# Three shared-expert parts moved to the last batch's end, second choices' sends written behind the shared expert, last norms in four groups

## The chip, the cores and the metric

The kernel runs on one core of a Trainium2 chip. The metric is the device time of one execution in microseconds (us); lower is better. TensorE is written PE, VectorE DVE, ScalarE ACT, GpSimd POOL and SyncE SP.

## The reference

One decoder layer for B = 4 batches of S = 1024 tokens of H = 256 features, float32 throughout, with a layer norm after each of three sublayers:

```python
x = _layernorm(x + self_attention(x))              # 16 heads, blended with two 4-head attentions
x = _layernorm(x + cross_attention(x, ctx, dist))  # 154 keys, a bias from log(dist)
x = _layernorm(x + moe(x))

# moe(h), 4096 tokens:
probs  = softmax(h @ gate_w)                       # 8 experts
w, idx = top_k(probs, 2); w = w / w.sum()          # two choices a token
y      = sum over the two choices: w * expert_idx(h)
y     += (silu(h @ ws_gate) * (h @ ws_up)) @ ws_down   # the shared expert, width 512
```

An expert has the form of the shared one: a gate and an up product of width 512, silu, and a product down to 256.

## The kernel before, in words

Tokens lie on the 128 partitions; a batch is NT = 8 tiles of 128 tokens, `ys[b]` is `[128, 8, 256]`. The four batches are worked through one after the other: self-attention, `close_sublayer` (output product, residual add, statistics, norm), the cross-attention's loop of 36 steps (`Cross.scores`, `flip`, `product`), and `end` (the cross-attention's `close_sublayer`, the transposes of the normed tokens, L135 with the copy L138, and the router's scores, L856, copied to `prob` at L863). Only then are all 4096 tokens routed.

Work that other engines leave room for is written as Python generators and stepped from inside these loops. `ahead` is such a generator: for batches 0 to 2 it holds the beginning of the next batch's self-attention (`begin`); in the last batch it is `shared_early(2)`, the shared expert for batch 2. `shared` yields 13 parts, called p0 to p12 here: p0 transposes the tokens, p1 to p4 are gate and up products of the first 512 tokens (L191), p5 to p8 those of the second 512, p9 to p12 the products down (L174), each followed by an add (L888) and a DMA to DRAM (L891). In the last batch p0 and p1 are stepped after the two `out_features` products, the others from `close_sublayer` and the cross loop, as the idle yields in `shared_early` space them.

Routing is a chain of small DVE operations (L1142 to L1239). It gives each of the 2 x 4096 choices a place in a DRAM array `scratch`, grouped by expert. `send(b, k)` writes two columns (`tail`: the token's number and the choice's weight) behind the 256 features in the tile `sent[b]` (`[128, 8, 258]`), and POOL then issues eight indirect DMAs, one for each tile of tokens, which scatter these rows to their places. Batches 0 and 1 have been kept in DRAM and are read again for that (`y0again`, `y1again`); in the profile `y` stands for batches 2 and 3. There are two rounds, k = 0 and k = 1; the second overwrites the two columns in the same tile. While that goes on, PE runs the shared expert for batch 0, batch 1 and the first half of batch 3 (`begin_result`), whose transposes read `sent[b][:, :, 0:H]`.

Then 72 tiles of 128 places are read back (`fetch`), go through their expert (`hidden`, `flip`, `down`) and are added to `result` by an indirect DMA. At the end `res[b]` is loaded from DRAM (L1397), the second half of batch 3's shared expert (`rest`) is finished on chip, and the last norm runs: `bn_stats` and `bn_aggr` on DVE (L1405, L1406), the square root on ACT (L1412), and the apply on ACT (L1422) or DVE (L1426), with one output DMA for each part (L1429).

The order of instructions on each engine is set by a scheduler from the order in which the program writes them; waits between engines are semaphores that the framework places by tile. [...]

Of the kernel before, what the change touches and what calls it, by code (L numbers as in the profile page):

```python
# [20 lines left out]
NT = S // P  # L21
# [19 lines left out]
def run(gen):  # L41
    for _ in gen:
        pass
# [3 lines left out]
def decoder_layer(ctx: ExitStack, tc: tile.TileContext, a, out):  # L47
# [53 lines left out]
    def rows(b):  # L101
        return result[b * S : (b + 1) * S, :].rearrange("(t p) d -> p t d", p=P)
# [57 lines left out]
    def shared(y, room, gated, add, together):  # L160

        x2T = room("x2T", [P, NC2, S])
        transpose_tokens(x2T, y)
        yield

        def down(tb, hid):
            for tp in range(2):
                ps = small()  # L170
                for i in range(2):
                    tok = 2 * tp + i
                    for f in range(NF):
                        nc.tensor.matmul(  # L174
                            ps[:, i * H : (i + 1) * H],
                            hid[:, f, tok * P : (tok + 1) * P],
                            shared_weights(2 * NC2 * D + f * H, H),
                            start=(f == 0),
                            stop=(f == NF - 1),
                        )  # L180
                add(ps, tb * 4 + 2 * tp)
                yield

        pend = []
        for tb in range(2):
            hid = room(f"hid{tb}", [P, NF, 512])
            for f in range(NF):
                ps = big()
                for i in range(2):
                    for c in range(NC2):  # L190
                        nc.tensor.matmul(  # L191
                            ps[:, i, :],
                            shared_weights((i * NC2 + c) * D + f * P, P),
                            x2T[:, c, tb * 512 : (tb + 1) * 512],
                            start=(c == 0),
                            stop=(c == NC2 - 1),
                        )
                gated(hid[:, f, :], ps)
                yield
            pend.append((tb, hid))  # L200
            if tb == 1 or not together:
                while pend:
                    yield from down(*pend.pop(0))


    with tc.tile_pool(name="wA", bufs=1) as wA, tc.tile_pool(name="work", bufs=2) as work:
# [581 lines left out]
        def close_sublayer(y, product):  # L788

            mv = work.tile([P, NT, nc.vector.BN_AGGR_DIM], F32, tag="mv", name="mv")  # L790
            for t in range(0, NT, 2):
                ps = small()
                for i in range(2):
                    product(ps[:, i * H : (i + 1) * H], slice((t + i) * P, (t + i + 1) * P))
                yy = y[:, t : t + 2, :]
                nc.vector.tensor_tensor(yy, ps.rearrange("p (t d) -> p t d", d=H), yy, ALU.add)
                ln_stats(y, t, mv, work)
                ln_stats(y, t + 1, mv, work)
                yield
            rstd = ln_rstd(mv, work, 0, NT)  # L800
            for t in range(NT):
                ln_apply(y, t, mv, rstd, t)
                if t % 2 == 1:
                    yield
# [67 lines left out]
        def shared_early(b):  # L872

            tags = {"x2T": "xT", "hid0": "v16", "hid1": "v64"}

            def room(name, shape):
                return work.tile(shape, F32, tag=tags[name], name="s" + name, bufs=1)

            def gated(dst, ps):

                sg = work.tile([P, 512], F32, tag="avs", name="sg")
                nc.scalar.activation(sg, ps[:, 0, :], AF.Tanh, scale=0.5)
                nc.vector.scalar_tensor_tensor(sg, sg, 1.0, ps[:, 0, :], ALU.add, ALU.mult)
                nc.vector.scalar_tensor_tensor(dst, ps[:, 1, :], 0.5, sg, ALU.mult, ALU.mult)

            def add(ps, t0):
                so = work.tile([P, 2, H], F32, tag="avs", name="so")
                nc.vector.tensor_tensor(  # L888
                    so, ps.rearrange("p (t d) -> p t d", d=H), ys[b][:, t0 : t0 + 2, :], ALU.add
                )  # L890
                nc.sync.dma_start(rows(b)[:, t0 : t0 + 2, :], so)  # L891

            for n, _ in enumerate(shared(ys[b], room, gated, add, True)):
                yield
                if n > 4:

                    yield
                    yield

        run(begin(0))  # L900

# [21 lines left out]
        for b in range(B):  # L923
# [82 lines left out]
                        ps, cm[:, c, tok], wo[:, c, :], start=(c == 0), stop=(c == NC2 - 1)  # L1006
                    )

            for _ in close_sublayer(y, self_out):
                next(ahead, None)  # L1010


            cT = work.tile([P, NC2, S2], F32, tag="cT", name="cT", bufs=1)
# [55 lines left out]
            for n in range(total + 4):  # L1069
                if n < total:  # L1070
                    xa.scores(n)
                    if n % 8 == 3 and n // 8 < NG - 1:
                        xa.project_q(n // 8 + 1)
                if 2 <= n < total + 2:
                    xa.flip(n - 2)
                if n >= 4 and n % 2 == 1:
                    xa.product(n - 4)
                next(ahead, None)
                xa.clock.step()
            xa.clock.finish()  # L1080
            cx4 = work.tile([P, NC2, S], F32, tag="cx", name="cx4", bufs=1)
            run(to_features(xtok, cx4, 1.0))
            run(ahead)
            behind = end(b, cx4)
            if b == B - 1:
                run(behind)


    NTT = B * NT
# [150 lines left out]


    def send(b, k):
        nc.gpsimd.tensor_copy(sent[b][:, :, H:RW], tail[:, k, b * NT : (b + 1) * NT, :])
        for t in range(NT):
            g = b * NT + t
            ins = nc.gpsimd.indirect_dma_start(
                out=scratch[:, :],
                out_offset=bass.IndirectOffsetOnAxis(ap=place[:, k, g : g + 1], axis=0),
                in_=sent[b][:, t, :],
                in_offset=None,  # L1250
            )
            tc.declare_no_dep(ins.ins, group="send", reason="places are unique")
            tc.add_to_no_dep_group("send", ins.ins)
# [91 lines left out]
        nc.scalar.activation(sl, ps[:, 0, :], AF.Silu)  # L1345
        nc.vector.tensor_tensor(dst, ps[:, 1, :], sl, ALU.mult)

    for k in range(2):
        for b in (2, 3, 0, 1):
            send(b, k)  # L1350

# [15 lines left out]
    for b in (0, 1):  # L1369
        run(begin_result(b, True))  # L1370
        nc.sync.dma_start(rows(b), res[b])
    b = B - 1
    nc.sync.dma_start(rows(b)[:, NT // 2 :, :], ys[b][:, NT // 2 :, :])
    rest = begin_result(b, False)
# [22 lines left out]
        nc.sync.dma_start(res[b], rows(b))  # L1397


    def statistics(parts, n):  # L1400
        mv = fw.tile([P, 16, nc.vector.BN_AGGR_DIM], F32, tag="mv", name="mv", bufs=3)
        for k, (b, t0) in enumerate(parts):
            for t in range(n):
                st = fw.tile([P, nc.vector.BN_STATS_DIM], F32, tag="bnst", name="bnst", bufs=3)
                nc.vector.bn_stats(st, res[b][:, t0 + t, :])  # L1405
                nc.vector.bn_aggr(mv[:, k * n + t, :], st)  # L1406
            yield mv

    def norm(parts, n, mv):
        m = n * len(parts)  # L1410
        rstd = fw.tile([P, 16], F32, tag="rstd", name="rstd", bufs=3)
        nc.scalar.activation(rstd[:, :m], mv[:, 0:m, 1], AF.Sqrt, bias=eps_t)  # L1412
        nc.vector.reciprocal(rstd[:, :m], rstd[:, :m])
        off = fw.tile([P, 16], F32, tag="off", name="off", bufs=3)
        nc.vector.scalar_tensor_tensor(
            off[:, :m], mv[:, 0:m, 0], -1.0, rstd[:, :m], ALU.mult, ALU.mult
        )
        for k, (b, t0) in enumerate(parts):
            for t in range(n):
                y, i = res[b][:, t0 + t, :], k * n + t  # L1420
                if i % 2 == 0:
                    nc.scalar.activation(  # L1422
                        y, y, AF.Identity, bias=off[:, i : i + 1], scale=rstd[:, i : i + 1]
                    )
                else:
                    nc.vector.tensor_scalar(  # L1426
                        y, y, rstd[:, i : i + 1], off[:, i : i + 1], ALU.mult, ALU.add
                    )
            nc.sync.dma_start(od[b][:, t0 : t0 + n, :], res[b][:, t0 : t0 + n, :])  # L1429

    halves = [(b, t) for b in range(B) for t in (0, NT // 2)][:-1]
    groups = [halves[:4], halves[4:]]
    stats = [statistics(g, NT // 2) for g in groups]
    mvs = [None, None]
    for f in range(NF):
        next(rest)
        g = stats[f // 2]
        for _ in range(2):
            mvs[f // 2] = next(g, mvs[f // 2])
    norm(groups[0], NT // 2, mvs[0])  # L1440
    norm(groups[1], NT // 2, mvs[1])
    for t0 in (NT // 2, NT // 2 + 2):
        next(rest)
        part = [(B - 1, t0)]
        norm(part, 2, next(statistics(part, 2)))
    run(rest)


# [27 lines left out]
```

## Time and profile before

| what | us |
|---|---|
| median of three runs | 3334.01 (3328.59 to 3344.21) |
| profiled execution | 3394.53 |
| its span | 3392.7 |
| PE busy | 3215.2 (95%) |
| DVE, ACT, POOL busy | 1670.2, 1612.6, 353.5 |
| mean granted PE clock | 0.973 |

The profile records one execution. A row of the timeline gives start and duration in us, then engine, line, operation, output and inputs, and in brackets the engine's idle time ahead of it with what ended it. A row of the waits gives the waiting instruction, what it waited for, the total, the number of times and the longest. A row of the windows gives for each stretch its length, the busy time and count of PE, its weight loads, DVE, ACT and POOL, the granted clock, the share of busy DMA engines and GB/s.

### The profile page before, as it was taken

How to read it: one execution, taken by the hardware profiler on the slowest of the kernel's cores; microseconds unless marked ns; L12 is line 12 of the kernel's file. 1: busy time of each engine (PE TensorE's matmuls, PEld its weight loads, DVE VectorE, ACT ScalarE, POOL GpSimd, SP SyncE). 2: the span in 40 equal slices, each digit the busy share in tenths (PEclk: the TensorE clock that was granted, in tenths of full speed). 3: DMA queues.
4: the chain of work that ended last, by engine and by line, in shares of the span. 5: the costliest groups of instructions: out<-in, count | busy, mean ns of one | idle time of the engine just before them, and what ended most of it. 6: DMA issues, size and time to landing. Idle time of an engine off the chain costs nothing.

```text
span 3392.7 us, 60480 instructions
## 1 busy us (share of the span) xinstructions
PE 3215.2 (95%) x25064; PEld 2047.2 (60%) x25064; DVE 1670.2 (49%) x3512; ACT 1612.6 (48%) x3168; POOL 353.5 (10%) x569
## 2 busy tenths in 40 slices
PE   8999999999999999999999999999999992999997
PEld 3655666566556665665576666555766761666664
DVE  3665555566645555666465555664555550111113
ACT  1555544465655444756554356655453630233333
POOL 1000000000000010000000100000000025133331
PEclk7999999999999999999999999999999996999999
DMA  7200000110000001100000100000000052122224
GB/s 230 76 2 1 1 1 3 45 35 31 2 1 1 1 18 36 45 15 2 1 1 1 38 16 21 14 2 11 1 10 1 14 203 91 41 46 46 47 44 120
DMA packets 83768, 111.36 MB, mean 33 GB/s; under 512 B 8896, under 2 KB 69672, under 8 KB 83496
## 3 DMA queue, kind: packets, MB, share of 16 engines
q1 hardware_dynamic: 70056, 89.60, 8.4%
q0 software_dynamic: 13440, 17.90, 3.2%
q8 instruction: 200, 3.28, 0.4%
q14 instruction: 72, 0.59, 0.1%
HBM read 59.10 MB, written 48.37 MB: 32 GB/s over the span
## 4 chain that ended last, share of the span: by engine, by line
PE 82%; DVE 10%; issue 3%; another core or an unknown queue 2%; ACT 1%; DMA 1%; POOL 0%; SPq 0%; DVEq 0%; POOLq 0%; ACTq 0%
PE big L483 8%; PE big L591 8%; PE big L1292 7%; PE one L627 7%; PE acc L645 7%; DVE mxp L490 7%; PE big L342 7%; PE one L541 7%; PE one L521 4%; PE acc L1318 4%; PE one L758 3%; PE big L191 3%; PE one L356 3%; PE big L723 3%; PE acc L777 2%
## 5 line engine op out<-in xcount | busy, mean ns | idle before, releaser
L490 DVE TENSOR_REDUCE mxp<-big 128x2 f32<-128x1024 f32 x512 | 610.8, 1219 | 347.5 <-PE acc L521 261.6
L483 PE MATMUL big<-k,q 31*128 31x512 f32 x2048 | 616.4, 639 | 34.3 <-DVE mxp L490 23.9
L521 PE MATMUL one<-q,k 32*128 32x256 f32 x2784 | 502.0, 398 | 0.0
L532 ACT ACTIVATE ex<-one 128x512 f32<-128x512 f32 x696 | 390.8, 600 | 220.5 <-PE acc L521 178.9
L323 DVE CUSTOM_DVE_ANT_0 prob<-big,zero_t 128x1024 f32<-128x1024 f32 x256 | 303.6, 1222 | 271.5 <-PE big L591 271.3
L521 PEld LDWEIGHTS one<-q,k 32*128 32x128 f32 x2784 | 331.6, 186 | 33.8 <-issue 2.5
L610 ACT ACTIVATE prob<-prob,nmx 128x1024 f32<-128x1024 f32 x256 | 293.0, 1152 | 21.9 <-DVE nmx L323 21.4
L483 PEld LDWEIGHTS big<-k,q 31*128 31x128 f32 x2048 | 186.3, 188 | 175.6 <-DVE mxp L490 88.8
L591 PE MATMUL big<-mk,mq 64*128 64x512 f32 x1024 | 284.0, 632 | 2.1 <-ACT ex L529 2.0
L632 ACT COPY pt<-one 128x512 f32<-128x512 f32 x256 | 137.8, 589 | 308.8 <-PE one L627 308.8
L627 PEld LDWEIGHTS one<-ident,prob 128*128 128x128 f32 x2048 | 220.4, 141 | 97.5 <-issue 91.8
L1292 PE MATMUL big<-wall,xt 128*128 x576 | 270.4, 593 | 0.5 <-ACT xt L1271 0.5
L521 PE MATMUL acc<-q,k 32*128 32x256 f32 x928 | 264.6, 404 | 0.0
L627 PE MATMUL one<-ident,prob 128*128 128x128 f32 x2048 | 256.3, 278 | 0.0
L541 PE MATMUL one<-ex,v 128*32 128x256 f32 x4096 | 250.9, 385 | 5.0 <-DVE q L400 5.0
L743 ACT ACTIVATE xs<-xs,xmx 128x154 f32<-128x154 f32 x512 | 175.1, 414 | 114.9 <-DVE xmx L323 114.9
L1302 DVE TENSOR_TENSOR hidr<-big,slr 128x512 f32<-128x512 f32 x72 | 49.8, 691 | 364.5 <-ACT slr L1300 364.5
L541 PEld LDWEIGHTS one<-ex,v 128*32 128x32 f32 x4096 | 120.2, 110 | 139.2 <-ACT ex L532 54.0
L634 DVE COPY pt<-one 128x512 f32<-128x512 f32 x256 | 164.3, 683 | 9.8 <-PE one L627 9.8
L591 PEld LDWEIGHTS big<-mk,mq 64*128 64x128 f32 x1024 | 99.8, 190 | 101.6 <-issue 79.5
L323 DVE CUSTOM_DVE_ANT_0 xs<-big,bias 128x154 f32<-128x154 f32 x512 | 132.6, 314 | 51.7 <-ACT avx L785 25.3
L554 POOL TENSOR_TENSOR avq<-avq 128x256 f32<-128x256 f32 x64 | 46.5, 726 | 1055.3 <-ACT avq L549 1055.3
(258 smaller groups left out, 4698.0 us busy)
## 6 DMA issues: line engine op xcount, KB each, us to landing
scratch<-empty SPq DMA_DIRECT2D x1, 9288.0 KB
xg<-scratch SPq DMA_DIRECT2D x72, 129.0 KB
q<-q_rows SPq DMA_DIRECT2D x16, 512.0 KB
k<-k_rows SPq DMA_DIRECT2D x16, 512.0 KB
y<-in_x_dram SPq DMA_DIRECT2D x4, 1024.0 KB
q_rows<-qh SPq DMA_DIRECT2D x8, 512.0 KB
k_rows<-kh SPq DMA_DIRECT2D x8, 512.0 KB
wall<-in_L_ffn_w_gate_dram SPq DMA_DIRECT2D x8, 512.0 KB
```

What stands on the lines that cost most here:

```text
L323: nc.vector.tensor_tensor_reduce(out=out, in0=ps, in1=bias, scale=-1.0, scalar=3.0e38, op0=ALU.add, op1=ALU.min, accum_out=low,)
L342: nc.tensor.matmul(ps[:, tb, :], w[:, c, lo : lo + P], xT[:, c, tb * 512 : (tb + 1) * 512], start=(c == 0), stop=(c == NC2 - 1),)
L483: nc.tensor.matmul(ps[:, jj, :], st["q"][r : r + MR, tok : tok + P], st["k"][r : r + MR, kb * 512 : (kb + 1) * 512], start=True, stop=True,)
L490: nc.vector.reduce_max(mxp[:, t, kb, 2 * pair : 2 * pair + 2], ps, axis=AX.X)
L521: nc.tensor.matmul(scs[jj][:, i * QW : (i + 1) * QW], st["k"][r : r + MR + 1, kc * P : (kc + 1) * P], st["q"][r : r + MR + 1, part * QW : ...
L532: nc.scalar.activation(ex[:, jj, :], scs[jj], AF.Exp, scale=1.0 / HD**0.5)
L541: nc.tensor.matmul(av[32 * j : 32 * j + 32, 0:QW], self.v[:, kc, h * VW : h * VW + 32], exs[kc // 2, j // 2][:, j % 2, i : i + QW], start= ...
L591: nc.tensor.matmul(pss[i][:, kb, :], q[r : r + MD, t * P : (t + 1) * P], k[r : r + MD, kb * 512 : (kb + 1) * 512], start=True, stop=True,)
L610: nc.scalar.activation(p, p, AF.Exp, bias=nmx[:, i : i + 1], scale=-1.0, accum_out=sm[:, t % 4, i : i + 1],)
L627: nc.tensor.transpose(ps[:, kc * P : (kc + 1) * P], probs[u][i][:, at : at + P], ident)
L645: nc.tensor.matmul(av[64 * i : 64 * i + 64, (t % 4) * P : (t % 4 + 1) * P], v[:, kc, h * MD : (h + 1) * MD], flipped[u][i][:, kc, :], star ...
L1292: nc.tensor.matmul(ps[:, g, :], xt[:, c * P : (c + 1) * P], wall[:, bass.ds(off + (g * NC2 + c) * D, D)], start=(c == 0), stop=(c == NC2 - 1),
```

## The change

Three parts of the program are changed.

A. `shared_early` returns the generator of `shared` itself, without idle yields. In the last batch `close_sublayer` steps it at every second yield (p2 to p5), the cross loop at n = 6, 12, 18 and 24 (p6 to p9), and `end` at its yields 4, 6 and 8 (p10 to p12). For the other batches the stepping stays as it was.

B. `send` copies the first choices' columns on DVE instead of POOL. Before the shared expert the program now writes only the first choices' sends; those of the second choices follow behind the shared expert of batches 0 and 1, for batches 2, 0, 3, 1.

C. The last norms are made in four groups of two half batches (8, 8, 8 and 4 tiles) where there were two of four and three, each with its statistics directly ahead of it. One tile in four is applied on DVE and three on ACT; before it was every second. In the two parts of batch 3's last half it stays one of two. The last four gate parts of the shared expert are written ahead of all of it and no longer interleaved with the statistics.

```diff
@@ shared_early
-            for n, _ in enumerate(shared(ys[b], room, gated, add, True)):
-                yield
-                if n > 4:
-
-                    yield
-                    yield
+            return shared(ys[b], room, gated, add, True)
@@ the loop over batches
-            for _ in close_sublayer(y, self_out):
-                next(ahead, None)
+            for n, _ in enumerate(close_sublayer(y, self_out)):
+                if b < B - 1 or n % 2 == 0:
+                    next(ahead, None)
@@
-                next(ahead, None)
+                if b < B - 1 or n in (6, 12, 18, 24):
+                    next(ahead, None)
                 xa.clock.step()
@@
-            run(ahead)
             behind = end(b, cx4)
             if b == B - 1:
-                run(behind)
+                for n, _ in enumerate(behind):
+                    if n > 3 and n % 2 == 0:
+                        next(ahead, None)
+            run(ahead)
@@ send
-        nc.gpsimd.tensor_copy(sent[b][:, :, H:RW], tail[:, k, b * NT : (b + 1) * NT, :])
+
+        eng = nc.gpsimd if k else nc.vector
+        eng.tensor_copy(sent[b][:, :, H:RW], tail[:, k, b * NT : (b + 1) * NT, :])
@@
-    for k in range(2):
-        for b in (2, 3, 0, 1):
-            send(b, k)
+    for b in (2, 3, 0, 1):
+        send(b, 0)
@@
     for b in (0, 1):
         run(begin_result(b, True))
         nc.sync.dma_start(rows(b), res[b])
+    for b in (2, 0, 3, 1):
+        send(b, 1)
@@ the last norms
-    def statistics(parts, n):
+    def norm(parts, n, on_dve):
         mv = fw.tile([P, 16, nc.vector.BN_AGGR_DIM], F32, tag="mv", name="mv", bufs=3)
...
-            yield mv
-
-    def norm(parts, n, mv):
+
         m = n * len(parts)
...
-                if i % 2 == 0:
+                if i % on_dve:
                     nc.scalar.activation(
@@
-    groups = [halves[:4], halves[4:]]
-    stats = [statistics(g, NT // 2) for g in groups]
-    mvs = [None, None]
-    for f in range(NF):
+    for _ in range(NF):
         next(rest)
-        g = stats[f // 2]
-        for _ in range(2):
-            mvs[f // 2] = next(g, mvs[f // 2])
-    norm(groups[0], NT // 2, mvs[0])
-    norm(groups[1], NT // 2, mvs[1])
+    for k in range(0, len(halves), 2):
+        norm(halves[k : k + 2], NT // 2, 4)
     for t0 in (NT // 2, NT // 2 + 2):
         next(rest)
-        part = [(B - 1, t0)]
-        norm(part, 2, next(statistics(part, 2)))
+        norm([(B - 1, t0)], 2, 2)
     run(rest)
```

## The prediction

> **What bounds the kernel now.** I read the page first (busy time by engine, busy slices, chain), then went into the three stretches that the change touches with the windows, the chain, the waits and the timeline. Two rows of the page's slices carry the first reading:
>
> ```profile
> PE   8999999999999999999999999999999992999997
> ...
> POOL 1000000000000010000000100000000025133331
> ...
> PE 82%; DVE 10%; issue 3%; another core or an unknown queue 2%; ACT 1%; DMA 1%; POOL 0%; SPq 0%; DVEq 0%; POOLq 0%; ACTq 0%
> ```
>
> PE sets the time: 3215.2 us busy of 3392.7. One slice, the 34th, breaks it with a 2 (each is 84.8 us, so it runs from 2799 to 2884), and it is the slice in which POOL is busiest. The waits between 2780 and 2870 us name the hole:
>
> ```profile
> ACT x2T L138 <- remote: 78.1, 2, 56.7
> PE big L191 <- ACT x2T L138: 42.9, 1, 42.9
> PE big L191 <- issue: 20.3, 1, 20.3
> DVE res L1360 <- issue: 25.3, 3, 20.4
> ```
>
> PE loses 42.9 + 20.3 = 63.2 us there waiting for two copies on ACT. What do those copies wait for? The timelines of PE, ACT, DVE and POOL:
>
> ```profile
> 2796.59 1.91 PE L135 MATMUL big<-ident,y1again 128*128 128x128 f32 x16
> ...
> 2840.31 1.01 ACT L138 COPY x2T<-big 128x1024 f32<-128x1024 f32 x1 [56.74 <-remote]
> 2862.71 1.01 ACT L138 COPY x2T<-big 128x1024 f32<-128x1024 f32 x1 [21.39 <-remote]
> ...
> 2797.53 0.69 DVE L1360 TENSOR_TENSOR res<-one,y0again 128x512 f32<-128x512 f32 x1 [6.96 <-PE one L174]
> 2818.61 0.69 DVE L1360 TENSOR_TENSOR res<-one,y0again 128x512 f32<-128x512 f32 x1 [20.39 <-issue]
> ...
> 2850.73 0.21 POOL L1243 COPY y1again<-tail 128x16 f32<-128x16 f32 x1
> 2860.15 0.97 POOL L1246 DMA_INDIRECT scratch<-y1again,place  x1 [0.30 <-issue]
> ```
>
> PE's transposes of y1again were through by 2798.5, yet the copies that only need them start at 2840.31 and 2862.71; the last down product of batch 0 was through near 2796.6, and its add starts at 2818.61. Four uses of PE's results in a row come 21.1, 21.7 and 22.4 us apart, while POOL issues 64 indirect sends back to back (2779.07 to 2861.1, 1.275 us each: 0.97 busy and 0.30 issue); once the last send is out it is over. No k=1 copy of `tail` stands in it: y1again's columns are written at 2850.73, 54 us after PE had started to read that tile. So the tail copies are not what these four wait for.
>
> Is this hole in the timed runs? The profiled execution took 3394.53 us (span 3392.7 and 1.8 around it), the median of the runs is 3334.01: 60.5 less. PE's rows without the hole end this stage 62.8 us earlier (2866.4 for 2929.2), which gives 3331.7, inside the runs' 3328.6 to 3344.2. I take it that the hole belongs to the profiled execution and that timed runs mostly lack it. This is the main choice of the forecast; the other reading is a rival below.
>
> **Part A: three parts of batch 2's shared expert moved to the last batch's end.** A part is 3.43 us of PE (L191, eight matmuls) or 3.45 (L174, eight). Before: p2 to p6 in `close_sublayer`, p7 to p12 in the cross loop. After: p2 to p5, then p6 to p9, and p10 to p12 in `end`. Both earlier places have PE full (48.83 busy of 50 us from 2560 to 2610; 118.36 of 122 from 2610 to 2732), so a part taken out is worth its whole length: −3.43 in `close_sublayer` (one less), −6.87 in the loop (net two less), less 0.2 us of start-up idle that p7 at n=1 filled. In `end` the three cost +10.35, of which this much lies in gaps:
>
> ```profile
> 2742.81 4.02 PE L135 MATMUL big<-ident,y 128*128 128x128 f32 x16 [2.88 <-DVE y L126]
> ...
> 2742.34 2.67 DVE L126 TENSOR_SCALAR y<-y,mv,rstd 128x256 f32<-128x256 f32 x8
> ```
>
> PE idles 2.88 us for the first normed tile, and its 16 transposes, paced by DVE's applies, take 4.02 where 16 unpaced take 1.91: 5.0 us of cover. Sum: −3.43 − 6.87 + 0.2 + 10.35 − 5.0 = −4.8 us (−3 if p10 alone fills, −5 at best). What is issued with them: three DVE adds (0.69 each, L888) and three 256 KB output DMAs on SP. On DVE one add stands between the reciprocal (L122) and the applies and waits for p10, two between the applies and the probability copy (L863); each is done before the PE scores (L856) behind p12 are. The third add also waits for the first part's DMA to leave its buffer. On SP they stand ahead of the expert-weight loads, which need the released buffer anyway and end near 2780, 80 us before an expert uses them.
>
> Behind it the routing keeps its order on DVE, but ACT now runs the routing softmax (L1144) between batch 0's two x2T copies: prob is 1.7 us earlier, the second copy later by two table loads. PE's first gate part pays +0.8 and the rank products (L1171/1172) wait where they ran free before: +1.05 net. A comes to −4.8 + 1.05 = −3.75 us on PE, and the sends start about 7.9 us earlier.
>
> Here a rule bears: by the trace a table load is 1.28 us (2754.99) with 0.02 us between the neighbour's end and it; the Trainium skill's "ScalarE: Activation LUTs", section "What ACT_TABLE_LOAD costs", adds a drain of about 1.38 us to each, 2.66 in all. One drain more ahead of the second copy would make A about −2.4; the rows show none, and I keep −3.75.
>
> **Part B: second choices sent behind the shared expert's code, the first ones' tail copies on DVE.** 64 sends before, 64 after, 1.275 us each, in another order; nothing on POOL stands between the two sets, since the k=1 copies have no reader to wait for. POOL loses four copies of 0.2 to 0.33 us; DVE gains four (nearest row: its 128x16 copies of L1186 at 0.17 us), 0.7 us in all ahead of the first shared products. First rule against it: the Trainium skill's "SBUF — State Buffer", section "SBUF: two separate sides", says that an fp32 SBUF-to-SBUF copy on DVE locks GpSimd out of the port with which it writes descriptors. Row: the sends keep 1.275 us under all of DVE's work from 2779 to 2819, though none of that is such a copy. By the rule the sends of y2 lose at most the other three copies, 0.5 us; by the row none. The first expert's gather (xg) lands 3.6 us after the last send (2864.7) and would be 7.9 us earlier; without the hole PE gets there at 2866.4. So B is worth 0 (−0.5 to +0.5), covered by PE's shared products; without that cover the send chain would be the bound, and it ends earlier too.
>
> **Part C: last norms in four groups, three quarters of the tiles on ACT.** Before, the output DMAs start late and then run at one rate:
>
> ```profile
> 3374.00:3376.00 2.00, 0.33 (x2) 0.30 (x3) 2.00 (x10) 0.00 (x0) 0.00 (x0) 1.00 0.00 0
> ...
> 3388.00:3390.00 2.00, 0.00 (x0) 0.00 (x0) 0.00 (x0) 0.00 (x0) 0.00 (x0) 0.50 1.09 385
> ...
> 3377.63 6.97 ACT L1422 ACTIVATE res<-res,off,rstd 128x256 f32<-128x256 f32 x14
> 3378.73 9.37 SPq L1429 DMA_DIRECT2D out_dram<-res  x9
> ```
>
> 4.19 MB from 3379.6 to 3390.5 at about 383 GB/s: the queue is the bound, its start is what counts. After: eight tiles' statistics (0.39 each on DVE) from 3365.0, sqrt, a Silu reload (1.28) and the last Silu (0.6), then six applies (0.498) on ACT: the first write near 3374.0, 5.6 us earlier. But ACT then has 23 applies (11.5 us) where it had 16, two table loads more (2.6 us), and waits for group 1's offsets, which stand on DVE behind 24 tiles of statistics (3378.55). Its last apply ends near 3387.85; 0.85 us from issue to data (as 3378.73 to 3379.6), 0.7 of data and the same tail put the end at 3389.5 to 3391. ACT takes the queue's place: C = 0 (−3 to +3; +2.7 with the page's drain at each of the two loads). DVE, with 9 applies where it had 16, is no cover for it.
>
> **The sum.** −3.75 + 0 + 0 = −3.75 on 3394.5, carried over to the median: 3334.0 − 3.8 = **3330 us**. Half a percent is 16.7 us, about what a measurement of this kernel can tell from no change.
>
> **Rivals.**
> - *As summed*, −12 to +8: chance 0.50.
> - *It doesn't do what it says*: the k=1 copies had nothing to wait for, p11 and p12 cover no idle time and the routing waits eat the rest: 3334, 0.14. For it: the copy at 2850.73. Against: 5.0 us of gap.
> - *The hole is real in the timed runs and goes.* For it: it stands in the one execution that the records show, and no load of instructions falls in it; fewer PE results have to reach other engines inside an earlier send train. Against: the 60.5 us difference, and that all 64 sends stay back to back. One late result less is −21 − 4: 3309; two, −42 − 4: 3288; all of it, −63 − 4: 3267. Faster, 0.22.
> - *A late result in the timed runs, slower.* The same delay, one mechanism, in a place where timed runs now escape it: x2T's copy (L138) of y1again or of batch 3's half while sends run. Moving the train 8 us against DVE and PE can let one result in; price 21 − 4 = +17 (3351), two +38 (3372). It decides from a delay of 20.5 us on. Against it: the median without a hole fits. 0.14.
>
> **Numbers.** Faster by over 0.5% 0.22, within it 0.64, slower 0.14. The range takes one late result either way and leaves out the larger ones: 3306 to 3356; the likeliest case alone is 3322 to 3342.
>
> **What would show.** A: PE's idle before the last L135 group of the batch under 1 us, 8 shared matmuls in it, probability copy 3 to 5 us earlier. B: 64 sends at 1.275 us, ordered k=0 then k=1 as before, no wait at the k=1 copies. C: first output DMA near 3374 of the old scale, ACT busy to the end. I am wrong if the timed median moves by more than 17 us, or if POOL's k=1 copies turn out to wait for PE.

## The result and the profile after

The changed kernel takes 3323.9 us (median of 20 executions, 3315.9 to 3334.9); the kernel before takes 3337.3 beside it. The ratio is 0.9965 (95% interval 0.9955 to 0.9975), so 8 to 15 us less. The forecast was 3330 us and 3.8 us less: the time lies in its range and within its half percent, but the gain is about three times as large as the sum said.

The two spans, 3392.7 and 3314.1 us, must not be compared as they stand. The hole of the profile before is not in the profile after. Slices of its page, and its chain:

```profile
PE   8999999999999999999999999999999999999997
...
POOL 1000000100000001000000010000000004433331
...
PE 84%; DVE 10%; issue 3%; ACT 2%; DMA 1%; POOL 0%; SPq 0%; ACTq 0%; DVEq 0%; POOLq 0%
```

PE has no slice with a 2, and no "unknown queue" stands in the chain, with POOL as busy as before. The waits of the changed kernel between 2780 and 2870 us, the same stretch in which PE lost 63.2 us before:

```profile
ACT x2T L138 <- PE big L135: 28.2, 2, 14.1
PE big L191 <- ACT x2T L138: 0.5, 2, 0.2
```

ACT's copies wait for their transposes alone, and PE for the copies 0.5 us. Was that the change? The experiments say no. Part A shows in PE's timeline at the end of the last batch:

```profile
2719.63 3.62 PE L844 MATMUL one<-xwo,cx 128*128 128x256 f32 x16
2723.09 7.07 PE L174 MATMUL one<-shwmc,shid 128*128 128x256 f32 x32
2729.99 1.04 PE L135 MATMUL big<-ident,y 128*128 128x128 f32 x8
2730.87 3.62 PE L174 MATMUL one<-shwmc,shid 128*128 128x256 f32 x16
2734.32 1.04 PE L135 MATMUL big<-ident,y 128*128 128x128 f32 x8
2735.20 0.29 PE L856 MATMUL one<-gw,x2T 128*128 128x8 f32 x2
```

None of these rows has an idle time in brackets. Where PE had waited 2.88 us for the norm and then been paced by it, it now works on the shared expert's products down (L174), and the 16 transposes run unpaced.

To see what a part is worth, I measure every profile from one point, the first self-output product of the last batch (L1005, L1000 after the change); all before it is the same program in each of these kernels. It begins anywhere between 2576 and 2591 us, also within one kernel (2576.5 in after, 2590.6 when the same kernel was profiled again), so single spans say nothing about a few us. The columns are differences of start times in PE's timeline: to the first cross-attention scores ("close"), on to the first L844 ("loop"), to the first router score ("end"), to batch 0's first shared product ("route"), to y1again's first transpose ("shared 0"), and to the first expert product ("shared 1, 3").

| kernel | close | loop | end | route | shared 0 | shared 1, 3 | sum |
|---|---|---|---|---|---|---|---|
| before, first profile | 36.44 | 111.80 | 13.94 | 7.07 | 42.87 | 133.47 | 345.59 |
| base_again | 36.43 | 113.42 | 13.79 | 7.48 | 43.41 | 70.91 | 285.44 |
| b_alone | 36.43 | 113.42 | 13.79 | 7.48 | 43.43 | 70.64 | 285.19 |
| c_alone | 36.44 | 113.39 | 13.81 | 7.49 | 43.47 | 70.87 | 285.47 |
| a_alone | 33.01 | 106.60 | 19.05 | 6.15 | 44.28 | 67.51 | 276.60 |
| after | 33.00 | 106.64 | 19.02 | 6.37 | 44.07 | 67.36 | 276.46 |
| a_behind | 33.00 | 106.54 | 13.87 | 19.15 | 41.62 | 67.36 | 281.54 |
| base_drop_2 | 36.44 | 113.30 | 13.92 | 7.48 | 43.52 | 67.36 | 282.02 |

A column of one profile can differ by 1.6 us within one kernel: the loop of the kernel before takes 111.80 us at a mean granted clock of 1.00 in the first profile and 113.42 at 0.98 in base_again.

### The profile page after: what moved, and what is told of

The parts are those of the page before. It is cut to its first block, busy times and chain, and to the rows that moved or that the text cites. A ratio compares the mean times of both kernels' runs of the same rounds, so it can differ in the third digit from the quotient of the medians.

```text
span 3314.1 us, 60483 instructions
## 1 busy us (share of the span) xinstructions
PE 3202.8 (97%) x25064; PEld 2042.6 (62%) x25064; DVE 1668.9 (50%) x3513; ACT 1619.0 (49%) x3179; POOL 352.2 (11%) x565
## 4 chain that ended last, share of the span: by engine, by line
PE 84%; DVE 10%; issue 3%; ACT 2%; DMA 1%; POOL 0%; SPq 0%; ACTq 0%; DVEq 0%; POOLq 0%
PE big L483 8%; PE big L591 8%; PE big L1293 7%; PE one L627 7%; PE acc L645 7%; DVE mxp L490 7%; PE big L342 7%; PE one L541 7%; PE acc L1319 4%; PE one L521 4%; PE one L758 3%; PE one L356 3%; PE big L191 3%; PE big L723 3%; PE acc L777 2%
## 5 line engine op out<-in xcount | busy, mean ns | idle before, releaser
L323 DVE CUSTOM_DVE_ANT_0 xs<-big,bias 128x154 f32<-128x154 f32 x512 | 132.6, 314 | 52.8 <-PE big L723 26.7
```

Source lines behind the costliest of these rows:

```text
L323: nc.vector.tensor_tensor_reduce(out=out, in0=ps, in1=bias, scale=-1.0, scalar=3.0e38, op0=ALU.add, op1=ALU.min, accum_out=low,)
```

## Experiments

**The kernel before once more, and each part alone.** base_again is the kernel before without an edit. The other three apply one part of the diff each.

> The kernel before, unchanged, executed and profiled once more. Theory 1 (the 63 us hole in the shared expert belonged to one execution): span near 3392.7 - 66 = 3327 us (66 with the slow clock behind the hole), x2T copies within 0.3 us of their transposes, ratio 1.000 within 0.002. Theory 2 (the hole is a property of this order of sends, whole or in part): the profile shows late x2T copies again while the sends run, span above 3340. Theory 3 (8 us of the gain arise in code that the change does not touch): the first score product of the last batch's cross loop (L723) moves by up to 8 us against 2620.9 without any edit.

> Part A alone: p2 to p12 restepped, sends and norms as before. Theory 1: PE 3.4 us earlier at the cross loop, about 3 us (2.5 to 4) earlier at y1again's transposes than in the kernel before, ratio 0.999. Theory 2: the same, and a hole in the profile. Theory 3 (layout or code placement of the edited program): 8 us or more earlier before the last batch.

> Part B alone: first choices' tail copies on DVE, second choices' sends written behind the shared expert. Theory 1: 64 sends at 1.275 us in one train, no hole, ratio 1.000 (0.9985 to 1.0015). Theory 2 (B takes away late PE results in the timed runs): ratio 0.9975 or less, at least 8 us. Theory 3: no gain behind the last batch's start.

> Part C alone: last norms in four groups, three tiles in four on ACT. Theory 1: 32.2 us from the result loads' issue to the end where the kernel before has 33.8, so -1.6 us, ratio 0.9995. Theory 2: the same, and a hole in the profile. The prediction: 0 (-3 to +3).

| kernel | median us | ratio to before | interval | span |
|---|---|---|---|---|
| base_again | 3334.0 | 0.9996 | 0.9985 to 1.0006 | 3332.3 |
| a_alone | 3326.2 | 0.9969 | 0.9956 to 0.9982 | 3324.9 |
| b_alone | 3336.4 | 1.0003 | 0.9993 to 1.0012 | 3330.3 |
| c_alone | 3335.7 | 0.9999 | 0.9987 to 1.0010 | 3334.3 |

Part A is the whole gain that the times can tell; B and C change nothing that they can tell. None of the four profiles has the hole, the unedited kernel and A and C among them: B did not remove it. Theory 2 falls. Theory 3 falls too: the code ahead of the last batch shifts by several us between executions of one kernel, and it shifted little in a_alone, which gains all the same.

But A gains more than theory 1 gave it: 8.8 us from the common point to the first expert (285.44 to 276.60) for the 2.5 to 4 expected. The table shows where the surplus is: 5.4 us are saved up to y1again's transposes, and 3.4 more behind them, in a stretch whose PE instructions A does not touch. POOL's last send and PE's timeline of base_again at its end:

```profile
2860.59 0.97 POOL L1246 DMA_INDIRECT scratch<-y1again,place  x1 [0.30 <-issue]
2865.42 0.44 PE L1269 MATMUL one<-ident,xg 128*128 128x128 f32 x2 [1.62 <-DMA xg<-scratch]
2868.02 2.93 PE L1292 MATMUL big<-wall,xt 128*128 x4 [2.16 <-issue]
```

PE has finished the shared expert and waits 1.62 us for the first gathered tile, and 2.16 more before its first expert product; what ended this second wait the profile does not show ("issue"). The gather waits for the last send: its DMA is issued at 2863.24, 1.7 us after the send's end, and in a_alone at 2857.60, 1.9 us after. In a_alone:

```profile
2854.75 0.97 POOL L1245 DMA_INDIRECT scratch<-y1again,place  x1 [0.30 <-issue]
2861.41 0.38 PE L1268 MATMUL one<-ident,xg 128*128 128x128 f32 x2
2862.40 1.96 PE L1291 MATMUL big<-wall,xt 128*128 x4 [0.61 <-ACT xt L1270]
```

No wait for xg, and 0.61 us where there were 2.16.

The table stops at the first expert product, but the waits cost more behind it:

```profile
2870.00:2880.00 10.00, 10.00 (x30) 4.93 (x29) 1.38 (x2) 2.70 (x6) 1.22 (x9) 0.89 0.14 45
```

This is base_again, with a granted clock of 0.89. Its first four expert products take 2.93 us where they take 1.96 in a_alone, and its third group of them starts 6.49 us behind the first (2874.51) for 4.81 (2867.21). That is 1.7 us more. From the common point to the end of the span base_again takes 749.7 us, b_alone 749.0, c_alone 748.8, a_alone 739.1 and after 737.6: A is worth 10.6 us in these traces, and its timed ratio of 0.9969 comes to 10.3.

**Is it the train of sends that bounds the first expert?** base_drop_2 leaves out the last eight sends (batch 1's second choices) and nothing else:

```diff
     for k in range(2):
         for b in (2, 3, 0, 1):
-            send(b, k)
+            if (b, k) != (1, 1):
+                send(b, k)
```

> The kernel before without the last eight sends, batch 1's second choices (left out of the computation), once more. Where no late results of PE lie in the train: 67.5 us from y1again's transposes to the first expert product instead of 70.9 if the train bounds the first expert in the kernel before, 70.9 if the shared products do. Where the hole is there: everything behind it about 10 us earlier, as the train ends 10.2 us earlier.

The stretch is 67.36 us, and PE's waits for xg are gone; all other columns stay within 0.2 us of base_again, and the third group of expert products follows 4.84 us behind the first. The ratio is 0.9982 (0.9973 to 0.9991), 3 to 9 us. So in the kernel before the train bounds the first expert by 3.5 us, and A takes that away by starting the train earlier: the first send stands 197.0 us behind the common point in base_again (2779.60) and 187.9 in a_alone (2773.68).

**Which of the two, PE or the train, bounds it once A is in?** a_behind puts p10 to p12 behind the router's scores; its edit against part A alone:

```diff
             if b == B - 1:
-                for n, _ in enumerate(behind):
-                    if n > 3 and n % 2 == 0:
-                        next(ahead, None)
+                run(behind)
             run(ahead)
```

> Part A with p10 to p12 behind the router's scores instead of between the end's steps. They then cover no idle time (PE reaches the shared expert of batch 0 about 5 us later than in part A alone), but the probabilities and with them the sends are about 5 us earlier. If PE bounds the first expert once A is in, this is 5 us slower than part A alone: ratio to the kernel before 0.9985. If the send train bounds it, this is 5 us faster than part A alone: 0.9955 or less. Where the hole is there, the train's end counts: about 11 us better than the kernel before, 0.997.

281.54 us for a_alone's 276.60: 4.9 slower, though its first send is the earliest of all (2761.92, 185.2 behind the common point; 2.7 us ahead of a_alone's, where 5 were expected). Ratio 0.9986 (0.9975 to 0.9998). PE bounds the first expert after A; an earlier train is worth no more, and the idle time at the end is worth what the prediction said:

```profile
2726.33 3.96 PE L135 MATMUL big<-ident,y 128*128 128x128 f32 x16 [2.88 <-DVE y L126]
2730.17 0.39 PE L856 MATMUL one<-gw,x2T 128*128 128x8 f32 x2
```

The wait of 2.88 us and the paced transposes are back.

**All of the change again.**

> All of the change, once more, beside the two others on one chip. Without the hole: 0.9965 as measured, 276.5 us from the last batch's self-output product to the first expert product. With the hole: the shared expert of batch 1 waits until the train is through, and the gain is what the train ends earlier against the first self-output product, 6 to 8 us: 0.998.

0.9959 (0.9945 to 0.9974), and 278.20 us for the stretch; 1.6 of the difference to after's 276.46 lies in the cross loop (108.23 for 106.64), where the program is the same and the mean granted clock was 0.97 for 0.98.

**A group of executions with the hole.** Four more kernels were run together. First base_drop and a_drop:

> The kernel before without the last eight sends, batch 1's second choices (left out of the computation; the same number of expert tiles is worked). If the send train bounds the first expert by 3.4 us in the kernel before, the stretch from y1again's transposes to the first expert product falls from 70.9 to about 67.5 us and PE's waits for xg (1.6) and behind it (2.2) go: ratio 0.999. If the shared expert's products bound it, as the prediction had it, nothing changes: 70.9 us.

> Part A alone, without the same eight sends (left out of the computation). If A has already moved the train out of the way, its 67.5 us from y1again's transposes to the first expert product stay, and base_drop and a_drop differ by A's part on PE alone, 5.4 us from the last batch's self-output product to the first expert. If some other effect of A makes the 3.4 us, both change alike.

Then a_loop, its edit against part A alone:

```diff
-                if b < B - 1 or n in (6, 12, 18, 24):
+                if b < B - 1 or n in (6, 10, 14, 18, 22, 26, 30):
                     next(ahead, None)
...
-                for n, _ in enumerate(behind):
-                    if n > 3 and n % 2 == 0:
-                        next(ahead, None)
+                run(behind)
```

> Part A with the cross loop holding p6 to p12 (n = 6, 10, ..., 30) and none in the end. If the gain is three parts taken into idle time of the end, the loop is 10.3 us longer than in part A alone (117 us), the end 5 us longer in PE idle but 10.3 shorter in work: 5 us of gain lost, and the send train later by as much, so the 3.4 us at the first expert come back too: 8 to 9 us slower than a_alone, ratio to the kernel before 1.000. If the gain comes from where the loop's parts stand, the ratio stays at 0.997.

And norm_half, its edit against the whole change:

```diff
-        norm(halves[k : k + 2], NT // 2, 4)
+        norm(halves[k : k + 2], NT // 2, 2)
```

> All of the change, but every second tile of the four norm groups on DVE instead of one in four. If ACT's 23 applies took the output queue's place, 17 applies end it about 2 to 3 us earlier: 29 to 30.5 us from the issue of the result loads to the end for 32.2; ratio 0.9955 to 0.996. If the group's statistics on DVE (or the late second square root) are what the applies wait for, it stays within 1 us of 32.2 or grows.

Beside them the kernel before took 3395 to 3416 us in all of its 43 executions; in the other groups none of its timed executions was above 3348. Kernels of one group share a chip. The ratios are to the kernel before on that chip:

| kernel | median us | ratio | interval |
|---|---|---|---|
| base_drop | 3391.1 | 0.9968 | 0.9957 to 0.9980 |
| a_drop | 3382.6 | 0.9945 | 0.9926 to 0.9965 |
| a_loop | 3402.9 | 1.0005 | 0.9995 to 1.0014 |
| norm_half | 3387.7 | 0.9960 | 0.9945 to 0.9975 |

All four profiles have the hole, norm_half with all three parts of the change in it too. ACT's and PE's timelines of norm_half:

```profile
2775.41 0.60 ACT L1346 ACTIVATE sl<-big 128x512 f32<-128x512 f32 x1 [2.84 <-issue]
2857.62 1.93 ACT L138 COPY x2T<-big 128x1024 f32<-128x1024 f32 x2 [81.61 <-remote]
...
2812.70 0.37 PE L135 MATMUL big<-ident,y1again 128*128 128x128 f32 x1 [2.43 <-issue]
2814.80 0.37 PE L135 MATMUL big<-ident,y1again 128*128 128x128 f32 x1 [1.73 <-issue]
...
2858.68 4.97 PE L191 MATMUL big<-x2T,shwca 128*128 128x512 f32 x6 [37.91 <-ACT x2T L138]
...
2848.65 0.97 POOL L1247 DMA_INDIRECT scratch<-y1again,place  x1 [0.30 <-issue]
```

Here not only the uses of PE's results are late: its transposes themselves start 0.7 to 2.8 us apart. The last send is through at 2849.62, and 8 us later all runs as usual. What the four tell: a_loop's 116.83 us of cross loop (117 expected) and 13.79 us of end show that the end's idle time is worth the 5.0 us; up to the first router score it takes 163.62 us, base_again 163.64 and a_alone 158.66. Of the stretch behind y1again base_drop and a_drop tell nothing, since the hole covers it; the first was repeated above, the second was not. In norm_half the end is 31.2 us behind the issue of the result loads (3354.47 to 3385.7) for 32.2 in after: 16 applies on ACT instead of 23 (the 17 of the expectation is a miscount) are worth 1 us, not 2 to 3, so ACT's applies alone do not set the end.

## Why the prediction was right or wrong

The range of 50 us and the class of half a percent would have held a gain of nothing as well, and the intervals above are about 0.1 percent wide to either side, not the half percent that the prediction took for the limit of the measurement. So that the number lies within them says little of the mechanism.

**Part A, the PE work: right but for the routing.** Less in `close_sublayer`: −3.43 forecast, −3.42 measured. Loop: −6.67 and −6.82, at a mean clock of 0.98 in both profiles. End: +5.35 and +5.26. The routing was to cost +1.05 and gave −0.5 (route −1.33, shared 0 +0.87). Much of this is clock: 30 router scores (L856) take 4.73 us in base_again, where the clock granted from 2750 to 2752 is 0.50, and 3.52 in a_alone; in the first profile, from which the forecast was made, they took 3.54. So this term is not resolved. Sum −5.4 for −3.75. (A part of L174 has sixteen matmuls in the rows, not eight; its 3.45 us stand.) The drain that the Trainium skill's "ScalarE: Activation LUTs", section "What ACT_TABLE_LOAD costs", adds does not show in the changed kernel's ACT timeline either:

```profile
2741.17 1.28 ACT L1143 ACT_TABLE_LOAD   x1
2742.46 0.42 ACT L1143 ACTIVATE prob<-prob 128x256 f32<-128x256 f32 x1
```

The activation follows the load within 0.01 us, and the copy ahead of it ends at 2741.14, 0.03 us before the load.

**Part B's cover: the step that failed.** "The first expert's gather (xg) lands 3.6 us after the last send (2864.7) ... without the hole PE gets there at 2866.4", so the train was called hidden. The 2866.4 was made by taking PE's idle time, 62.8 us, off a stretch of 132.6 us. But that stretch holds work at a slow granted clock, which the subtraction kept in. PE's rows and two windows of the first profile, and PE's row of base_again for the same products:

```profile
2841.38 2.07 PE L191 MATMUL big<-x2T,shwca 128*128 128x512 f32 x2 [42.88 <-ACT x2T L138]
2863.78 3.78 PE L191 MATMUL big<-x2T,shwca 128*128 128x512 f32 x4 [20.33 <-issue]
...
2840.00:2850.00 10.00, 2.07 (x2) 0.50 (x2) 0.00 (x0) 1.01 (x1) 7.56 (x9) 0.50 0.28 99
2860.00:2870.00 10.00, 6.22 (x10) 2.80 (x11) 0.30 (x1) 1.61 (x2) 1.41 (x4) 0.61 0.12 40
...
2799.25 2.90 PE L191 MATMUL big<-x2T,shwca 128*128 128x512 f32 x6 [0.23 <-ACT x2T L138]
```

With its last two matmuls this first gate part took 6.7 us at clocks of 0.50 and 0.61, and 3.6 in base_again. The undisturbed stretch of base_again takes 66.7 us (2797.11 to 2863.80), 3.1 less than the 69.8 that I had used. PE is there 1.6 us before the tile, not 1.7 us behind it, and the earlier train, which I had worked out (7.9 us; 9.1 measured) and then costed at nothing, pays 3.4 us. With it A is −8.8 us up to the first expert product, and −10.6 to the end with the slow clock that the waits had left there; the timed ratio of A says −6 to −15.

**Part B itself: right.** No wait at the k=1 copies, one train, 1.275 us for each send, 1.0003 alone. DVE's four copies did not slow it: in b_alone the last of them starts at 2777.76 and the first send at 2778.01, which waits for it ("DVE y1again L1245"). So no copy runs while sends do, and the port rule of the Trainium skill's "SBUF — State Buffer", section "SBUF: two separate sides", was not put to the test.

**Part C: right at 0, and in the traces as worked out.** From the issue of the result loads to the end it takes 33.8 us in base_again, 32.7 in c_alone and 32.2 in after. The first output DMA is issued 14.0 us behind the result loads (19.8 in base_again; the forecast's first write at 3374.0 lies 15.1 behind them), and then the queue stands idle, as a row of the changed kernel's windows and two of ACT's timeline show:

```profile
3300.00:3302.00 2.00, 2.00 (x11) 1.77 (x10) 2.00 (x12) 1.30 (x4) 0.00 (x0) 1.00 0.00 0
...
3299.73 0.30 ACT L1412 ACTIVATE rstd<-mv,eps_t 128x8 f32<-128x8 f32 x1 [0.85 <-DVE mv L1408]
3300.74 6.01 ACT L1422 ACTIVATE res<-res,off,rstd 128x256 f32<-128x256 f32 x12 [0.70 <-DVE off L1415]
```

Nothing is moved from 3300 to 3302, when ACT has waited for DVE's statistics and offsets and has only begun the next applies. The prediction had named this wait: offsets 19.7 us behind the result loads, 18.8 measured. In norm_half, with fewer applies on ACT and more on DVE, ACT waits for DVE in five places after its first applies, 4.2 us in all. That fits its gain of only 1 us; no run takes the wait away alone.

**The hole: right for the timed runs, wrong as to what it is.** Taking the timed runs as free of it was right. But it does not belong to one execution: by their times it was in every execution of one group and in none of the others. The first profile is a single execution whose chip is not on record. The rivals that made it a matter of this change, its removal or a new late result, both fall: it comes and goes without an edit, and with all three parts in it stays.

## What to carry to other kernels

A stretch that follows a long stall can't be cleared by subtracting the stall: the slow clock that came with it (3.1 us here) is still in the rows, and a margin of 2 us between two chains is then not known. When two chains meet within such a margin, cost the change on both, and treat the one called hidden as worth up to its whole lead. Filling an idle time of PE with work from a stage in which PE is full paid the idle time here (5.1 us for 5.0 counted), and it paid again because the chain behind it started earlier. A wait's cost does not end with the wait either: count it up to where the clock is back.

## What the runs showed that was not expected

In one group of executions, and in the first profile, ACT and DVE use PE's results up to 64 us late while POOL issues 56 or 64 indirect DMAs back to back, and PE's own instructions can start 0.7 to 2.8 us apart; both end with the train. It costs about 65 us: shared 1, 3 takes 125 to 140 us instead of 67 to 71. The kernel has no wait there that explains it. It held for all executions of the group, which share a chip, so it may go with the chip or with the time at which they ran; this was not separated. Its cause was not found, and a train broken up by pauses was not tried.
